# Order of products, refills, sums and decays in the first stage of a two-layer Mamba, FP4 and attention kernel

## The chip, the cores and the metric

The kernel runs on one core of one Trainium2 chip. The metric is the device time of one execution in microseconds; the time before is the median of three runs. One execution was taken by the hardware profiler, and all views of the profile come from it. A core has a matrix engine (PE, with its weight loads shown as PEld), a vector engine (DVE), an activation engine (ACT), a general engine (POOL) and a queue engine for transfers (SP). Each runs its own instructions in order and waits for the others by semaphores.

## The reference

The inputs are eight sequences of 512 tokens with 256 channels, all in fp32. Two layers follow each other; the change touches the first alone:

```
xn = layernorm(x)
x  = x + mamba(xn) + fp4_ffn(xn)          # first stage of the kernel
xn = layernorm(x)
x  = x + block_sparse_attention(xn) + local_transformer(xn)   # second stage
```

The Mamba block, for each sequence:

```
u, z  = split(xn @ W_in.T)                 # 512 channels each
u     = silu(causal_conv4(u) + conv_b)
dt, B, C = split(u @ W_xproj.T)            # 16 each
delta = softplus(dt @ W_dt.T + b_dt)
h[t]  = exp(delta[t] * A) * h[t-1] + delta[t] * u[t] * B[t]     # 16 states a channel
y[t]  = sum over states of h[t] * C[t]
out   = ((y + D * u) * silu(z)) @ W_out.T
```

The feed-forward block quantizes its input, its weights and its hidden layer to FP4 in blocks of 16 and returns to fp32: `down(fp4(silu(x @ Wg.T) * (x @ Wu.T)))` with 704 hidden channels.

## The kernel before

**Stages.** Two stages run one after the other, each with its own buffers. The first (lines 117 to 855) takes the eight sequences ("batches", b) through Mamba and feed-forward and writes x1 to memory; the second (from line 858) does the rest. In the first stage all engine instructions keep the order in which the program issues them (class `Ordered`, line 45).

**The scan loop.** The loop at line 826 counts steps g. A step handles two of the 16 states of one 128-channel chunk c, so a chunk takes 8 steps, a batch 32 (`STEPS`) and all batches 256. The work of one step:

- `fetch_c(g + 2)`: SP fetches two rows of C, spread over 128 partitions (three buffers, cb).
- `scan(g)`: DVE runs two scans of 512 tokens into hh (four buffers), from the decays da and the inputs bu.
- `decay(g + 2)`: ACT makes two decays da = exp(delta * A) (six buffers, three steps' worth).
- `inputs(g + 1)`, in odd steps alone: PE refills bu, by 16 small matrix products, for the next two steps. bu lies in PSUM and has one buffer, so the refill waits for the odd step's scans.
- `times_c(g)`: POOL multiplies hh by C.
- `sum_states(g)`: PE adds hh into y by 8 transposes with accumulation (PSUM, one buffer). Before, sums are issued in odd steps: that of g - 2 ahead of the strands and that of g - 1 behind them; the first one of a chunk comes later, in its even step.

**Strands.** All other work of the stage consists of generators that are advanced once per step by `step()` (line 800): `head` (layer norm, input projection, convolution, silu, x-projection, softplus; it makes the next batch ready), `ffn` (quantization and feed-forward), `z` and `finish` (the gate and the end of one chunk), `output`, and at the start the preparation of weights and tables. `begin` sorts them by rank: z and finish first, then output, the softplus chains and diagonals, head, ffn. `skewed` turns a list of stages into a pipeline over units: in one advance, each unit in flight does one stage. A stage is written as (function, tiles freed, tiles taken): products go to PSUM tiles of the pool pmm, of which there are three (`MM`), and a strand whose next advance would need more than three held tiles is passed over in that step.

**behind.** A function given to `behind` is kept in the list `late` and issued at the end of the same `step()`, when all strands have been advanced. The line-53 helper records every instruction, so the profile shows L53 for the first stage and the tiles tell the work apart: ps_in, cv (projection and convolution), ps_z, z (the gate), ps_dt, delta, du, e (softplus and delta * u), ps_gu, h (gate and up products of the feed-forward), ps_i, ht, ps_d (turning and the down product), q_ (quantization), ps_xp, xd (x-projection), ps_y, u (end of a chunk), ps_tr, xt, xqt (turned inputs).

**Readiness.** Before scan g the loop makes sure that the delta and du of step g + 2 are ready (`able`, line 815); as long as they are not, it advances the strands alone (line 831).

Of the kernel before, what the change touches and what calls it, by code (L numbers as in the profile page):

```python
# [9 lines left out]
FP = mybir.dt.float32  # L10
BF = mybir.dt.bfloat16
AF = mybir.ActivationFunctionType
# [5 lines left out]
P = 128  # L18
NB, L, D = 8, 512, 256
NT = L // P  # L20
KC = D // P
DI, NS, DR = 512, 16, 16
# [36 lines left out]
def tile_kernel(ctx: ExitStack, tc: tile.TileContext, a: dict, out: bass.AP):  # L59
# [57 lines left out]
    with ExitStack() as s0:  # L117
# [50 lines left out]
        def behind(f):  # L168


            late.append(f)
# [201 lines left out]
        def head(b):  # L373
# [41 lines left out]
            def project(c, _):  # L415
                ps = pmm.tile([P, L], FP, tag="mm", name="ps_in")
                for k in range(KC):
                    pe.matmul(
                        ps, w_in[:, k, c * P : (c + 1) * P], xt[:, k, :], start=(k == 0), stop=(k == KC - 1)
                    )  # L420
                cv = rot.tile([P, L], FP, tag="cv", bufs=2, name="cv")
                behind(lambda: act.activation(
                    cv, ps, AF.Identity, scale=conv_w[:, c, 3:4], bias=conv_b[:, c : c + 1]
                ))
                return ps, cv

            def tap(cv, ps, c, s):
                dve.scalar_tensor_tensor(
                    cv[:, s:], ps[:, : L - s], conv_w[:, c, 3 - s : 4 - s], cv[:, s:], ALU.mult, ALU.add
                )  # L430

            def taps(c, st):
                ps, cv = st
# [11 lines left out]

            while b - 3 in u_:
                yield 0, 0
            stages = [(project, 0, 1), (taps, 1, 0), tanh, silu]
            yield from skewed(range(NC - 2), stages, 2)
            while b - 2 in u_:  # L450
                yield 0, 0
# [46 lines left out]
            def rank(c):  # L498
                ps = pmm.tile([P, L], FP, tag="mm", name="ps_dt")
                pe.matmul(ps, w_dt[:, c * P : (c + 1) * P], xd, start=True, stop=True)  # L500
                behind(lambda: parts(c, ps))
                return ps

            def parts(c, ps):
                dt = delta[b, c] = w1.tile([P, L], FP, tag="delta", bufs=HELD, name="delta")
                w = du[b, c] = w1.tile([P, L], FP, tag="du", bufs=HELD, name="du")
                act.activation(dt, ps, AF.Relu, bias=b_dt[:, c : c + 1])
                act.activation(ps, ps, AF.Abs, bias=b_dt[:, c : c + 1])
                act.activation(ps, ps, AF.Exp, scale=-1.0)
                act.activation(w, ps, AF.Copy, bias=1.0)  # L510

            def rests(c, ps):
                e = rot.tile([P, L], FP, tag="e", bufs=3, name="e")
# [16 lines left out]
            def turned(c, _):  # L530
# [10 lines left out]
            by = pool if b else dve  # L541
            begin(diagonals(), 2)
            stages = [
                (lambda c, _: rank(c), 0, 1), (rests, 1, 0), logs, deltas, (turned, 0, 0, 1),
            ]
            for c in range(NC):
                k = b * NC + c - HELD
# [6 lines left out]
        def ffn(b):  # L554

            xn = made[b][0]

            def first(i, _):
                return xn[:, 2 * i : 2 * i + 2, :].rearrange("p t d -> p (t d)")

            scales, *stages = fp4_stages(P, 2 * D)
            yield from skewed(range(2), [lambda i, _: scales(i, first(i, _)), *stages], 3)
            yield 0, 0
            while b - 1 in busy:
                yield 0, 0
            busy.add(b)
            xqt = one.tile([P, KC, L], FP, tag="xqt", name="xqt")

            def turn_x(k, _):
                ps = pmm.tile([P, L], FP, tag="mm", name="ps_tr")  # L570
                for t in range(NT):
                    pe.transpose(ps[:, t * P : (t + 1) * P], xn[:, t, k * P : (k + 1) * P], ident)
                behind(lambda: act.copy(xqt[:, k, :], ps))

            yield from skewed(range(KC), [(turn_x, 0, 0, 1)], 1)
            quantized.add(b)
            n = FI // 2

            def product(t, w, cols):
                ps = pmm.tile([P, L], FP, tag="mm", name="ps_gu")  # L580
                for k in range(KC):
                    pe.matmul(
                        ps[:, :n], xqt[:, k, t * P : (t + 1) * P], w[:, k, cols],
                        start=(k == 0), stop=(k == KC - 1),
                    )
                return ps

            def gate_up(half):
                cols = slice(half * n, (half + 1) * n)

                def gate(t, h):
                    ps = product(t, w_g, cols)
                    behind(lambda: act.activation(h[:, cols], ps[:, :n], AF.Tanh))
                    return h, ps

                def up(t, st):
                    h, ps = st
                    dve.scalar_tensor_tensor(h[:, cols], h[:, cols], 1.0, ps[:, :n], ALU.add, ALU.mult)
                    if half and t == NT - 1:
                        busy.remove(b)  # L600
                    return h, product(t, w_u, cols)

                def both(t, st):
                    h, ps = st
                    dve.tensor_tensor(h[:, cols], h[:, cols], ps[:, :n], ALU.mult)
                    return h

                return gate, up, both

            def down(t, ht):  # L610
                ps = pmm.tile([P, L], FP, tag="mm", name="ps_d")
                for c in range(NI):
                    pe.matmul(ps[:, :D], ht[:, c, :], w_d[:, c, :], start=(c == 0), stop=(c == NI - 1))
                return ps

            def add(t, ps):
                x = xs[b]
                dve.tensor_tensor(x[:, t, :], x[:, t, :], ps[:, :D], ALU.add)

            def begin_(t, _):  # L620
                return gate0(t, q.tile([P, FI], FP, tag="q_src", bufs=4, name="h"))

            (gate0, up0, both0), (gate1, up1, both1) = gate_up(0), gate_up(1)
            stages = [
                (begin_, 0, 1), (up0, 1, 1), (lambda t, st: gate1(t, both0(t, st)), 1, 1), (up1, 1, 1), (both1, 1, 0),
                *fp4_stages(P, FI),
                *to_inner(lambda t: hts[t % 2]), (down, 0, 1), (add, 1, 0),
            ]
            for i, need in enumerate(skewed(range(NT), stages, 5)):
                if i == len(stages) - 6:  # L630
                    yield from own_x(b)
                yield need
            done(b)
# [106 lines left out]
        def z(b, c):  # L740
            yield 1, 1
            ps = pmm.tile([P, L], FP, tag="mm", name="ps_z")
            for k in range(KC):
                pe.matmul(
                    ps, w_in[:, k, DI + c * P : DI + (c + 1) * P], made[b][1][:, k, :],
                    start=(k == 0), stop=(k == KC - 1),
                )
            t = rot.tile([P, L], FP, tag="z", bufs=2, name="z")
            behind(lambda: act.activation(t, ps, AF.Tanh))
            yield 0, -1  # L750
            z_[b, c] = t
            dve.scalar_tensor_tensor(t, t, 1.0, ps, ALU.add, ALU.mult)
            through.add((b, c))
# [43 lines left out]

        ranks = {output: 1, head: 3, ffn: 4, fp4_weights: 5, rotary_tables: 5}

        def step():  # L800
            brief = 0
            for s, (peak, kept, *briefly) in list(active.items()):
                if held[0] + peak <= MM:
                    held[0] += kept
                    brief += sum(briefly)
                    active[s] = next(s, None)
                    if active[s] is None:
                        del active[s]
            for f in late:
                f()  # L810
            late.clear()
            held[0] -= brief
# [9 lines left out]
            fetch_c(k)  # L822
            decay(k)
        inputs(0)
        g = summed = 0
        while g < total or active or any(s >= g for s in starts):
            clock[0] = g
            for f, *args in starts.pop(g, []):
# [5 lines left out]
                fetch_c(g + 2)  # L834
            if now:
                scan(g)
            if g + 2 < total:
                decay(g + 2)
            if g % 2 and g + 1 < total:
                inputs(g + 1)  # L840
            while summed < min(g - 1, total):
                sum_states(summed)
                summed += 1
            if g % 2:
                gates = {g - (b * NC + c + 1) * (NS // 2) : (b, c) for b in range(NB) for c in range(NC)}
                for k, f in ((-3, z), (1, finish)):
                    if k in gates:
                        begin(f(*gates[k]), 0)
            step()
            if now:  # L850
                times_c(g)
            if g % 2 and 0 <= summed < min(g, total) and summed % (NS // 2):
                sum_states(summed)
                summed += 1
            g += 1


# [679 lines left out]
```

## Time and profile before

| what | value |
|---|---|
| device time, median of three runs | 3360.19 us (3358.26 to 3360.55) |
| device time of the profiled execution | 3363.26 us |
| its span, first to last instruction | 3361.3 us |
| mean granted TensorE clock | 0.948 |
| first scan starts, last scan ends | 49.7 and 1335.4 us |
| first load of x1 by the second stage | 1359.0 us |
| busy over the span: PE, DVE, ACT, POOL | 2984.9, 2263.7, 1562.5, 1545.1 us |

The costliest groups of the first stage, from the page (busy and mean per instruction; matrix products count two instructions in the trace for one in the program, except transposes):

| group | instructions | busy us | mean ns |
|---|---|---|---|
| POOL hh times C | 256 | 612.6 | 2401 |
| DVE scan hh | 512 | 592.3 | 1199 |
| ACT decay da | 512 | 338.4 | 715 |
| PE sums y | 2048 | 315.9 | 306 |
| PE refill bu | 4096 | 185.4 | 328 |

Busy times of PE overlap in the pipeline, so a group's mean is longer than its share of time: 16 instructions of a refill pass in 1.17 us at the quickest. A line of the view of waits gives the engine that waited and for what it would have gone on with, the releaser, the time in total, how often and the longest. A line of the timeline gives start, duration, engine, line, operation, result and inputs, shapes and number, and in brackets the idle time before it with its releaser.

### The profile page before, as it was taken

Reading aid. Unit: us, or ns where it says so; the run is one execution under the profiler, and the core shown is the slowest. Engines: PE = TensorE matmul, PEld = TensorE weight load, DVE = VectorE, ACT = ScalarE, POOL = GpSimd, SP = SyncE. Lnnn points to the kernel's source line nnn. Section 1 sums busy time; section 2 is a strip of 40 time slices with the busy share of each in tenths; the row PEclk is TensorE's granted clock in tenths of the full one; section 3 lists DMA queues with packets and bytes.
Section 4 is the critical chain, followed back from the end, with each engine's and each line's share of the span. In section 5 each row is a group of like instructions: output and inputs, shape, how many; then the busy total and the mean of one; then the engine's idle time right before and its main releaser. Section 6 shows DMA issues by size and latency. Waiting matters only on the chain.

```text
span 3361.3 us, 50387 instructions
## 1 busy us (share of the span) xinstructions
PE 2984.9 (89%) x19012; PEld 1836.9 (55%) x19012; DVE 2263.7 (67%) x4426; ACT 1562.5 (46%) x3399; POOL 1545.1 (46%) x1103
## 2 busy tenths in 40 slices
PE   5577798887888778899999999999999999999998
PEld 3455566665666566455555545545545545545545
DVE  6878787888888787556466566556557556556544
ACT  5464646474656553234244334334334434433533
POOL 2786777786868797223123123223213312312412
PEclk7778998998899998999999999999999999999999
DMA  3333333333333343210110111110110110110110
GB/s 111 111 104 108 117 104 124 119 117 117 114 120 109 118 138 118 85 50 35 46 49 35 46 54 37 48 50 32 65 34 32 65 34 32 65 33 32 59 34 7
DMA packets 93801, 244.42 MB, mean 73 GB/s; under 512 B 9848, under 2 KB 46712, under 8 KB 93560
## 3 DMA queue, kind: packets, MB, share of 16 engines
q1 hardware_dynamic: 92408, 237.01, 20.8%
q10 hardware_dynamic: 1152, 4.19, 0.3%
q8 instruction: 151, 2.47, 0.3%
q14 instruction: 90, 0.74, 0.1%
HBM read 231.48 MB, written 9.70 MB: 72 GB/s over the span
## 4 chain that ended last, share of the span: by engine, by line
PE 62%; DVE 17%; ACT 4%; issue 3%; POOL 2%; DMA 1%; DVEq 0%; POOLq 0%; ACTq 0%; SPq 0%
PE ps_qkv L1190 10%; DVE hh L53 6%; PE ps_g L1369 5%; PE ps_a L1369 4%; PE ps_wo L1333 3%; PE bu L53 3%; PE y L53 3%; PE lo L1303 3%; PE ps_y L1404 3%; PE ps_w L1387 3%; PE pt L1289 3%; PE ps_ls L1242 2%; PE ps_gu L53 2%; PE ps_st L1103 2%; DVE nm L1056 2%
## 5 line engine op out<-in xcount | busy, mean ns | idle before, releaser
L53 POOL TENSOR_TENSOR hh<-hh,cb 128x1024 f32<-128x1024 f32 x256 | 612.6, 2401 | 263.7 <-DVE hh L53 147.8
L53 DVE TENSOR_TENSOR_SCAN hh<-da,bu 128x512 f32<-128x512 f32 x512 | 592.3, 1199 | 65.3 <-PE bu L53 62.9
L53 PE MATMUL bu<-bd,du 32*128 32x128 f32 x4096 | 185.4, 328 | 253.7 <-DVE hh L53 240.5
L53 ACT ACTIVATE da<-delta,a_neg 128x512 f32<-128x512 f32 x512 | 338.4, 715 | 19.4 <-DVE hh L53 17.3
L53 PEld LDWEIGHTS bu<-bd,du 32*128 32x128 f32 x4096 | 158.3, 226 | 310.4 <-issue 207.5
L53 PE MATMUL y<-ident,hh 128*128 128x128 f32 x2048 | 315.9, 306 | 7.0 <-ACT delta L53 6.4
L1280 POOL TENSOR_TENSOR pr<-pr,lrs 128x512 f32<-128x512 f32 (+1 forms) x256 | 234.9, 934 | 177.4 <-DVE lrs L1278 137.6
L53 PEld LDWEIGHTS y<-ident,hh 128*128 128x128 f32 x2048 | 266.5, 158 | 55.7 <-issue 27.3
L1209 POOL TENSOR_TENSOR r<-r,r 128x512 f32<-128x512 f32 x128 | 163.0, 1273 | 285.4 <-DVE r L1207 242.9
L1261 ACT ACTIVATE pr<-ps_ls,nm 128x256 f32<-128x256 f32 (+1 forms) x512 | 222.0, 449 | 122.9 <-DVE nm L1255 116.7
L1205 DVE TENSOR_TENSOR r<-ps_qkv,tab 128x512 f32<-128x512 f32 x128 | 88.2, 689 | 200.1 <-ACT sq L1204 198.1
L1107 ACT ACTIVATE pt_e<-ps_st 128x512 f32<-128x512 f32 x320 | 166.8, 597 | 107.4 <-PE ps_st L1101 101.2
L945 POOL MEMSET sa<- 128x1 f32 x16 | 1.6, 99 | 449.9 <-DVE sf L1391 356.9
L1375 ACT ACTIVATE gl<-ps_g,b 128x512 f32<-128x512 f32 x96 | 65.9, 687 | 305.8 <-PE ps_g L1369 305.8
L1150 POOL TENSOR_TENSOR x1s<-x1s,bsum 128x256 f32<-128x256 f32 x32 | 23.2, 725 | 371.8 <-DVE x1s L1149 371.8
L1255 DVE CUSTOM_DVE_ANT_0 ps_ls<-ps_ls,mask 128x256 f32<-128x256 f32 (+1 forms) x512 | 184.1, 421 | 6.7 <-PE ps_ls L1242 5.8
L1369 PE MATMUL ps_g<-hn,wf 128*128 128x512 f32 x384 | 184.7, 604 | 4.0 <-DVE hn L1358 2.6
L1190 PE MATMUL ps_qkv<-wqkv,sf 128*128 128x512 f32 x384 | 182.4, 608 | 0.0
L1190 PE MATMUL ps_qkv<-wqkv,s 128*128 128x512 f32 x384 | 180.7, 606 | 0.0
L1376 DVE SCALAR_TENSOR_TENSOR ht<-ps_a,b,gl 128x512 f32<-128x512 f32 x80 | 60.0, 750 | 157.5 <-PE ps_a L1369 157.5
L1289 PE MATMUL pt<-ident,pr 128*128 128x128 f32 x896 | 131.3, 282 | 32.8 <-POOL pr L1280 28.1
L1369 PE MATMUL ps_a<-hn,wf 128*128 128x512 f32 x320 | 150.4, 592 | 0.0
(225 smaller groups left out, 6324.6 us busy)
## 6 DMA issues: line engine op xcount, KB each, us to landing
cb<-c_d SPq DMA_DIRECT2D x256, 512.0 KB, 3.7
wqkv<-in_wqkv SPq DMA_DIRECT2D x16, 1536.0 KB, 7.3
wf<-in_wf SPq DMA_DIRECT2D x16, 1408.0 KB, 6.3
wf<-in_wf SPq DMA_DIRECT2D x16, 768.0 KB, 4.7
tab<-tab SPq DMA_DIRECT2D x16, 512.0 KB, 3.5
wo<-in_wo SPq DMA_DIRECT2D x16, 512.0 KB, 3.7
xl<-in_x SPq DMA_DIRECT2D x8, 512.0 KB, 4.7
x<-in_x SPq DMA_DIRECT2D x8, 512.0 KB, 4.4
```

Source lines behind the costliest of these rows:

```text
L53: return self.tc.keep_in_program_order(getattr(self.engine, name)(*args, **kwargs))
L1107: act.activation(pt, banks[g], AF.Exp)
L1190: pe.matmul(ps, shifted(s, k, t * P, P), wqkv[:, k, i * IN : (i + 1) * IN], start=(k == 0), stop=(k == KC - 1),)
L1209: pool.tensor_tensor(r1[:, i], r1[:, i], r2, ALU.add)
L1255: last = dve.tensor_tensor_reduce(at, at, msk[:, 2 * P - nk :], -1.0, 3e38, ALU.add, ALU.min, nm[:, i : i + 1])
L1261: act.activation(pr[:, at], banks[r][:, at], AF.Exp, bias=nm[:, i : i + 1], scale=-1.0, accum_out=rs[:, i : i + 1],)
L1280: pool.tensor_tensor(ph, ph, rs.unsqueeze(2).to_broadcast([P, 2, nk]), ALU.mult)
L1289: pe.transpose(pt[:, j * P : (j + 1) * P], pr[:, j * P : (j + 1) * P], ident)
L1303: pe.matmul(o[r * LD : (r + 1) * LD, i * P : (i + 1) * P], lv[:, keys[j], h * LD : (h + 1) * LD], prts[r][:, (i * nkt + j) * P : (i * nkt ...
L1333: pe.matmul(ps, wo[:, c, m * P : (m + 1) * P], ot[:, c, :], start=(c == 0), stop=(c == IN // P - 1),)
L1369: pe.matmul(dst, wf1[:, k, off : off + P], hn[:, k, :], start=(k == 0), stop=(k == KC - 1))
L1387: pe.matmul(ps, wf2[:n, c, m * P : (m + 1) * P], ht[c][:n], start=(c == 0), stop=(c == NHC - 1),)
```

## The change

Five things change, all in the first stage.

1. Five activations that were issued `behind` their products, in the same step, become stages of their own: the first tap of the convolution (`tap0`), the softplus's four activations (`parts`), the tanh of both gate halves (`tanh0`, `tanh1`) and the tanh of z. They are issued one step after the product, and the DVE operation that frees the PSUM tile one step later than before.
2. In a step of the scan loop the strands are advanced directly after `scan(g)`, ahead of the refill `inputs(g + 1)` and of the sums.
3. The decays of step g + 2 are issued after the strands' own instructions and ahead of the functions in `late` (through the new argument `between`).
4. Every step g issues the sum of step g - 2, at its end, behind `times_c(g)`.
5. `finish` begins at k = 2, one step later; both z and finish are looked for in every step.

```diff
                     pe.matmul(
                         ps, w_in[:, k, c * P : (c + 1) * P], xt[:, k, :], start=(k == 0), stop=(k == KC - 1)
                     )
-                cv = rot.tile([P, L], FP, tag="cv", bufs=2, name="cv")
-                behind(lambda: act.activation(
-                    cv, ps, AF.Identity, scale=conv_w[:, c, 3:4], bias=conv_b[:, c : c + 1]
-                ))
-                return ps, cv
+                return ps
...
+            def tap0(c, ps):
+                cv = rot.tile([P, L], FP, tag="cv", bufs=2, name="cv")
+                act.activation(
+                    cv, ps, AF.Identity, scale=conv_w[:, c, 3:4], bias=conv_b[:, c : c + 1]
+                )
+                return ps, cv
...
-            stages = [(project, 0, 1), (taps, 1, 0), tanh, silu]
+            stages = [(project, 0, 1), tap0, (taps, 1, 0), tanh, silu]
...
             def rank(c):
                 ps = pmm.tile([P, L], FP, tag="mm", name="ps_dt")
                 pe.matmul(ps, w_dt[:, c * P : (c + 1) * P], xd, start=True, stop=True)
-                behind(lambda: parts(c, ps))
                 return ps
...
-                (lambda c, _: rank(c), 0, 1), (rests, 1, 0), logs, deltas, (turned, 0, 0, 1),
+                (lambda c, _: rank(c), 0, 1), parts, (rests, 1, 0), logs, deltas, (turned, 0, 0, 1),
...
                 def gate(t, h):
-                    ps = product(t, w_g, cols)
-                    behind(lambda: act.activation(h[:, cols], ps[:, :n], AF.Tanh))
-                    return h, ps
+                    return h, product(t, w_g, cols)
+
+                def tanh(t, st):
+                    h, ps = st
+                    act.activation(h[:, cols], ps[:, :n], AF.Tanh)
+                    return st
...
-                (begin_, 0, 1), (up0, 1, 1), (lambda t, st: gate1(t, both0(t, st)), 1, 1), (up1, 1, 1), (both1, 1, 0),
+                (begin_, 0, 1), tanh0, (up0, 1, 1), (lambda t, st: gate1(t, both0(t, st)), 1, 1), tanh1, (up1, 1, 1), (both1, 1, 0),
...
+            yield 0, 0
             t = rot.tile([P, L], FP, tag="z", bufs=2, name="z")
-            behind(lambda: act.activation(t, ps, AF.Tanh))
+            act.activation(t, ps, AF.Tanh)
             yield 0, -1
...
-        def step():
+        def step(between=lambda: None):
...
                     if active[s] is None:
                         del active[s]
+            between()
             for f in late:
                 f()
...
             if now:
                 scan(g)
-            if g + 2 < total:
-                decay(g + 2)
+            gates = {g - (b * NC + c + 1) * (NS // 2) : (b, c) for b in range(NB) for c in range(NC)}
+            for k, f in ((-3, z), (2, finish)):
+                if k in gates:
+                    begin(f(*gates[k]), 0)
+            step(lambda: g + 2 < total and decay(g + 2))
             if g % 2 and g + 1 < total:
                 inputs(g + 1)
-            while summed < min(g - 1, total):
-                sum_states(summed)
-                summed += 1
-            if g % 2:
-                gates = {g - (b * NC + c + 1) * (NS // 2) : (b, c) for b in range(NB) for c in range(NC)}
-                for k, f in ((-3, z), (1, finish)):
-                    if k in gates:
-                        begin(f(*gates[k]), 0)
-            step()
             if now:
                 times_c(g)
-            if g % 2 and 0 <= summed < min(g, total) and summed % (NS // 2):
-                sum_states(summed)
-                summed += 1
+            if 0 <= g - 2 < total:
+                sum_states(g - 2)
             g += 1
```

More of the change, by code (lines that the diff above doesn't have):

```diff
@@ L510, in parts @@
                 act.activation(w, ps, AF.Copy, bias=1.0)
+                return ps
             def rests(c, ps):
@@ L606, in both @@
                     return h
-                return gate, up, both
+                return gate, tanh, up, both
             def down(t, ht):
@@ L621, in begin_ @@
                 return gate0(t, q.tile([P, FI], FP, tag="q_src", bufs=4, name="h"))
-            (gate0, up0, both0), (gate1, up1, both1) = gate_up(0), gate_up(1)
+            (gate0, tanh0, up0, both0), (gate1, tanh1, up1, both1) = gate_up(0), gate_up(1)
             stages = [
-                (begin_, 0, 1), (up0, 1, 1), (lambda t, st: gate1(t, both0(t, st)), 1, 1), (up1, 1, 1), (both1, 1, 0),
+                (begin_, 0, 1), tanh0, (up0, 1, 1), (lambda t, st: gate1(t, both0(t, st)), 1, 1), tanh1, (up1, 1, 1), (both1, 1, 0),
                 *fp4_stages(P, FI),
@@ L824, in tile_kernel @@
         inputs(0)
-        g = summed = 0
+        g = 0
         while g < total or active or any(s >= g for s in starts):
```

## The prediction

> **What bounds the kernel now.** I read first the slices of the page, to find the stage that the change touches.
>
> ```profile
> PE   5577798887888778899999999999999999999998
> DVE  6878787888888787556466566556557556556544
> ACT  5464646474656553234244334334334434433533
> POOL 2786777786868797223123123223213312312412
> PEclk7778998998899998999999999999999999999999
> ```
>
> A slice is 84 us. The change lies in the first 16, where no engine is full: DVE stands highest, PE and POOL beside it, and the granted TensorE clock is below full. From slice 17 on PE is at 9 and the clock is full; nothing of the change reaches there. Next, the busy time of the stretch that holds the scans and of its tail (columns: stretch, length, busy PE, PEld, DVE, ACT, POOL, clock, DMA, GB/s).
>
> ```profile
> 47.40:1338.00 1290.60, 1008.17 (x8214) 771.94 (x8215) 1067.69 (x1272) 726.98 (x1189) 982.98 (x564) 0.89 0.34 115
> 1338.00:1361.00 23.00, 19.29 (x104) 15.71 (x102) 9.72 (x17) 4.91 (x10) 11.60 (x13) 1.00 0.09 21
> ```
>
> DVE works 1067.7 of 1290.6 us, so 222.9 us are idle, and DVE issues in program order: the stage lasts as long as DVE's work plus DVE's waits. The third view says what these waits are (us in total, times, longest), for DVE in that stretch, and for PE over the run:
>
> ```profile
> DVE hh L53 <- PE bu L53: 62.9, 59, 2.4
> DVE h L53 <- ACT h L53: 47.5, 23, 3.7
> DVE e L53 <- ACT du L53: 32.7, 21, 3.3
> DVE cv L53 <- ACT cv L53: 25.4, 15, 3.2
> DVE x L53 <- PE ps_d L53: 15.7, 14, 1.9
> DVE z L53 <- ACT z L53: 10.2, 11, 3.2
> DVE h L53 <- PE ps_gu L53: 4.0, 7, 2.1
> DVE bd L53 <- PE ps_bt L53: 2.7, 3, 1.3
> ...
> PE bu L53 <- DVE hh L53: 240.5, 90, 12.0
> ```
>
> The rows h, e, cv and z are the pattern "product, activation behind it in the same step, DVE in the next": 47.5 + 32.7 + 25.4 + 10.2 = 115.8 us. The first row is the refill of bu, which an odd step issues for the next two scans; today DVE waits little for it, because PE stands ready at it (last row: PE is the one that waits). The timeline shows one such place.
>
> ```profile
> 664.93 0.49 DVE L53 TENSOR_TENSOR h<-h,ps_gu 128x352 f32<-128x352 f32 x1
> 665.16 1.17 PE L53 MATMUL bu<-bd,du 32*128 32x128 f32 x32 [1.38 <-DVE hh L53]
> ...
> 666.49 2.33 DVE L53 TENSOR_TENSOR_SCAN hh<-da,bu 128x512 f32<-128x512 f32 x2 [1.06 <-PE bu L53]
> ...
> 690.50 2.09 PE L53 MATMUL bu<-bd,du 32*128 32x128 f32 x32 [2.36 <-DVE hh L53]
> ```
>
> The bu tile has one buffer: a refill starts at the odd scans' end, takes 1.17 us (2.09 where the clock is low), and the next scan follows at once if DVE has too little of its own to do meanwhile.
>
> **The change, part by part.** All instructions stay; their order and their step change. The counts below are from the order in which the two built programs issue their instructions, with what each waits for. Durations are rows of the trace.
>
> *(a) Activations a step behind their products.* DVE's operation now comes two steps after the product, its activation one. The 115.8 us go. I take -100, because ACT still ends each step on copies of products of that step (du, ht, xt) and may hand some of it on. Ends: -116 and -50.
>
> *(b) Products ahead of the refill.* PE issues in order. In an odd step it now runs all strands' products before the refill; the sums and the next step's products queue behind. A product that waits for a DVE operation of its own step (it takes the PSUM tile that this operation frees) holds the refill. In the changed order 50 of 124 odd steps have such a product ahead of the refill. Step 161 shows it: after the scans DVE has one operation (e, 0.68 us); ps_d's six matmuls wait for it (2.59 us in the before's rows), then comes the refill (1.17): it ends 4.44 us after the scans, DVE is done after 0.68, and waits 3.76. In the old order the refill is first and ends at 1.17. I did this sum for every odd step (mean DVE durations; products 0.68 us for a ps_gu instruction, 0.43 for ps_d, 0.47 for ps_o, 0.94 for ps_in and ps_z, 1.02 for ps_dt, 0.60 for four transposes; only the products from the first blocked one on count): DVE's waits come to 21.7 us in the old order, where the trace has 62.9, and to 125.5 us in the new one, in 89 steps, with a mean end of 2.34 us. The sum is low because the mean refill is 185.4 / 128 = 1.45 us, not 1.17, 24% more. 24% of 2.34 is 0.56, times 89 is 50: 125.5 + 50 = 175, less the 62.9 of today, +113. Ends: +63 (the bare sum) and +213 (the steady odd steps 131 to 163 sum to 27.1, 1.6 each; 2.16 with the 0.56, times 128 is 276, less 62.9).
>
> The low clock is seen in the two refills above, 1.17 and 2.09 us. The Trainium skill, page "TensorE: Matmul & The Clock Gate", part 1, says that the array runs at half clock after an idle window of about 3.4 us and at full clock after a busy one; by that rule shorter idle gaps of PE would speak for the change, and with all refills at 1.17 the +113 would be +63.
>
> *(c) PSUM tiles held longer.* project, rank, z and both gates now keep their tile for two steps instead of one; the stage has three tiles, and a strand whose turn finds none skips a step. The built order shows the result: the x-projection of later batches comes 3 to 9 steps later (step 120 instead of 111 for batch 4, 212 instead of 207 for batch 7), and at steps 30, 94 and 126 the next batch's du is not ready, so 3, 1 and 4 steps of the strands alone are issued with no scan in them. I walked the four at step 126: from the end of scan 125 the softplus chain (two rounds of four activations of 0.6, Ln between two table loads of 1.28, three POOL operations of 1.28, transposes, copy) lasts about 14.5 us, in which DVE has 9.5 us of work: 5 idle. The three at 30 alike, 2 for the one: +12. Ends: +5, and +32 (eight times 4 us, nothing covered).
>
> "Perfetto Trace Analysis" of the skill, section "Optimization Strategy", says that a bubble that repeats can mean too little PSUM for the next tile; it speaks against holding tiles longer, and has no price.
>
> *(d) The tail.* The same lag makes the loop end at step 275 instead of 265: ten more steps of the feed-forward strand after the last scan. The ten of today last 23 us with 9.7 us of DVE work: 2.3 a step, 1.3 idle. Ten more: +14 (their DVE work is taken out of the loop). Ends +5 and +26.
>
> *(e)* Start before the first scan, pipeline one stage deeper in two places: +2 (0 to +5).
>
> *(f) Other waits of DVE for products of the step before* (ps_d, ps_gu, ps_bt and smaller, 25 us with those not shown): products start earlier, but queue behind others: -5 (-25 to +15).
>
> *(g) At nothing.* The decays go behind the strands' activations: a scan needs them two steps on, and ACT is busy 56%; were that cover gone, each late pair costs up to its 1.33 us. Three more table loads (80 for 77) lie there too, 3.8 us if bare. The copy of y and the finish move a step back: the first sum of the next channel waits for that copy in its own (even) step, where no refill is due; bare, some 1 us at 32 places. sums at g - 2 instead of pairs: the h tile has four buffers, so a scan needs the sum issued two steps before. SP's fetches of C keep their place; the store of x on ACT's queue and the x load on SP's move with the lag and are waited for by the sum of x alone.
>
> Sum: -100 + 113 + 12 + 14 + 2 - 5 = +36 us on the span of 3361.3: 3397; the median of the runs, 3360.2, lies 1.1 lower: **3396 us**.
>
> **Rivals.** *The refill fits (faster).* PE idles 240 us at the refill today and would use it for the products, so the refill is late only by the bare sum: -116 + 63 + 5 + 5 - 25 = -68, 3292, at best; -100 + 63 + 12 + 14 + 2 - 5 = -14, 3346, with the middle values of the rest; 3320 between them. For it: PE's idle time and the low clock. Against: the 50 blocked steps, where PE can't run ahead. It decides where DVE's waits for bu stay below 62.9 + 77 = 140 us, since all other terms make -77.
>
> *The refill becomes the chain (much slower).* PE, late from the even step's blocked products, is late at every odd one: (b) at +213, +136 in all, 3496. For it: the steady batches, where 15 of 17 odd steps are late by the sum; PE busy 78% of the stretch already. Against: early batches show less.
>
> *A wash.* (a) and (b) cancel and (c) and (d) are covered: within 0.2%, 3353 to 3367, about what a measurement of this kernel can tell from no change.
>
> **How the numbers follow.** Forecast, 3367 to 3440: 0.50. Much slower: 0.20. Refill fits: 0.25. Wash: 0.05. Faster 0.25, same 0.05, slower 0.70. The range leaves out the lower half of the faster case and the upper half of the much slower one: 3320 to 3490. The likeliest case's own range is 3367 to 3440.
>
> **What would show it.** DVE's waits for ACT's h, du, cv and z under 20 us in all (a); its wait for PE's bu between 140 and 220 us (b), with PE waiting less at bu and more at products for DVE; du late at the batch changes of the first batches only (c); some 23 us more between the last scan and the second stage's first load (d). Wrong I am if bu stays below 140 us, or if waits for ACT stay.

## The result and the profile after

The changed kernel takes 3476.23 us (median of four runs, 3474.44 to 3477.64), the one before 3360.37 beside it: ratio 1.0345 (1.0327 to 1.0363). The forecast was slower, 3396 us with a range of 3320 to 3490: the sign was right and the time lies in the range, but the loss is +116 us where +36 was forecast. The profiled execution has a span of 3473.8 us, 112.5 more than before.

| stretch of the span, us | before | after | change |
|---|---|---|---|
| first scan to last scan's end | 1285.7 | 1369.7 | +84.0 |
| from there to the second stage's first load of x1 | 23.6 | 51.1 | +27.5 |
| second stage | 2002.3 | 2003.3 | +1.0 |

The slices of the page after (86.8 us each):

```profile
PE   5567777787777788799999999999999999999998
DVE  6978776777677778565655655565466556556544
PEclk7788998998899899989999999999999999999999
```

The first stage now fills nearly all of slice 17, where it ended a sixth into it before, and DVE shows mostly sevens where it had sevens and eights. The busy time of the two first-stage stretches of the table, after (columns as in the prediction):

```profile
47.40:1419.40 1372.00, 1035.65 (x8152) 744.32 (x8152) 1059.55 (x1252) 728.74 (x1181) 970.65 (x557) 0.89 0.33 108
1419.40:1470.50 51.10, 38.77 (x165) 29.62 (x164) 20.22 (x34) 8.10 (x20) 20.78 (x19) 0.90 0.08 23
```

DVE is busy 1059.6 us in the loop (1066.8 before, in the same stretch up to its last scan) and idle 312.4 (221.2 before). So the loop's +84 is +91 of waits, less 7 of work that moved into the tail. The granted clock of the loop is 0.89 as before: PE doesn't run slower. DVE's waits in the loop, after:

```profile
DVE hh L53 <- PE bu L53: 227.9, 91, 6.1
DVE x L53 <- PE ps_d L53: 15.5, 6, 6.0
DVE hh L53 <- ACT da L53: 13.7, 5, 6.2
DVE e L53 <- ACT du L53: 10.4, 5, 4.9
DVE z L53 <- ACT z L53: 9.5, 2, 6.0
...
DVE h L53 <- ACT h L53: 1.6, 2, 0.9
```

The four rows of ACT that the shift was to remove fell from 115.8 to 21.5 us (cv is gone). The wait for the refill rose from 62.9 to 227.9, and further scans (the row hh <- ACT da and smaller ones) wait 35.0 us where they waited 2.2; what these rows are is taken up under (g). PE's waits over the run show the other side:

```profile
PE bu L53 <- DVE hh L53: 70.5, 30, 9.3
PE ps_gu L53 <- DVE h L53: 30.5, 18, 3.8
...
PE ps_in L53 <- DVE cv L53: 25.2, 8, 4.0
PE ps_gu L53 <- DVE x L53: 13.4, 9, 5.4
...
PE ps_d L53 <- DVE z L53: 12.9, 5, 5.0
```

PE waited 240.5 us at the refill before, 70.5 now. In exchange the stage's products wait, for DVE, ACT and POOL: between 47 and 1440 us, all such rows of PE, without those of the sums, come to 260 us, and to 24 before. 214 of the 260 are waits for DVE. The releasers (h, cv, x, z) are mostly not inputs of the product that waits: they are the DVE operations that read the PSUM tile that it takes over. One such place, from the timeline after:

```profile
1011.85 1.95 PE L53 MATMUL ps_in<-xt,w_in 128*128 128x512 f32 x4 [2.26 <-DVE u L53]
...
1012.65 2.32 DVE L53 TENSOR_TENSOR_SCAN hh<-da,bu 128x512 f32<-128x512 f32 x2
...
1013.86 1.35 PE L53 MATMUL ps_gu<-w_g,xqt 128*128 128x352 f32 x4
...
1015.04 1.04 PE L53 MATMUL y<-ident,hh 128*128 128x128 f32 x8
...
1015.92 2.76 PE L53 MATMUL ps_d<-w_d,ht 128*128 128x256 f32 x12
...
1018.60 1.17 PE L53 MATMUL bu<-bd,du 32*128 32x128 f32 x32
...
1019.94 2.33 DVE L53 TENSOR_TENSOR_SCAN hh<-da,bu 128x512 f32<-128x512 f32 x2 [4.97 <-PE bu L53]
```

In the even step ps_in waits 2.26 us for DVE. That makes ps_i (in a line left out), ps_gu and the sum late, so that PE only comes to the even step's sum (y) as the odd step's scans end, at 1014.97 (1012.65 + 2.32). Then follow the odd step's six products ps_d, which wait for nothing, then the refill, 3.6 us after the scans. DVE waits 4.97 us. In the old order the refill stands ahead of these sums and of ps_d.

### The profile page after: what moved, and what is told of

Its sections match the earlier page's. It is cut to its first block, busy times and chain, and to the rows that moved or that the text cites. A ratio compares the mean times of both kernels' runs of the same rounds, so it can differ in the third digit from the quotient of the medians.

```text
span 3473.8 us, 50299 instructions
## 1 busy us (share of the span) xinstructions
PE 3033.5 (87%) x19012; PEld 1823.8 (53%) x19012; DVE 2267.7 (65%) x4426; ACT 1567.8 (45%) x3402; POOL 1543.3 (44%) x1103
## 4 chain that ended last, share of the span: by engine, by line
PE 58%; DVE 14%; ACT 3%; issue 2%; POOL 1%; DMA 0%; DVEq 0%; ACTq 0%; POOLq 0%
PE ps_qkv L1191 10%; PE ps_g L1370 5%; DVE hh L53 5%; PE ps_a L1370 4%; PE ps_wo L1334 3%; PE lo L1304 3%; PE ps_y L1405 3%; PE ps_w L1388 3%; PE pt L1290 2%; PE ps_gu L53 2%; PE bu L53 2%; PE ps_ls L1243 2%; PE y L53 2%; DVE nm L1057 2%; PE pt_qk L1182 1%
## 5 line engine op out<-in xcount | busy, mean ns | idle before, releaser
L53 DVE TENSOR_TENSOR_SCAN hh<-da,bu 128x512 f32<-128x512 f32 x512 | 592.5, 1201 | 263.2 <-PE bu L53 227.9
L53 PE MATMUL y<-ident,hh 128*128 128x128 f32 x2048 | 300.6, 295 | 8.8 <-ACT delta L53 8.7
L53 PEld LDWEIGHTS y<-ident,hh 128*128 128x128 f32 x2048 | 254.5, 153 | 57.9 <-issue 31.4
L53 PE MATMUL bu<-bd,du 32*128 32x128 f32 x4096 | 171.1, 310 | 71.3 <-DVE hh L53 70.5
L53 PEld LDWEIGHTS bu<-bd,du 32*128 32x128 f32 x4096 | 145.1, 211 | 128.6 <-issue 92.6
```

The lines of the kernel that those rows point to most:

```text
L53: return self.tc.keep_in_program_order(getattr(self.engine, name)(*args, **kwargs))
```

## The experiments

Ratios are to the kernel before, run beside each on the same chip, with 95% intervals.

**The order and the shift, separately.** Four kernels fill a table of two questions: do the five activations come a step behind, and where does the refill stand?

*The change with the refill first again:*

```diff
             if now:
                 scan(g)
+            if g % 2 and g + 1 < total:
+                inputs(g + 1)
...
             step(lambda: g + 2 < total and decay(g + 2))
-            if g % 2 and g + 1 < total:
-                inputs(g + 1)
```

> The changed kernel with one move undone: the refill of bu is issued ahead of the strands again; activations a step behind, decays and sums stay as changed. Theory A (the products ahead of the refill are the cost: DVE waited 227.9 us for bu in the changed kernel, 62.9 before): DVE's wait for bu falls to 60 to 110 us, and the time by 110 to 160 us, to 3315 to 3365 us. Theory B (the longer hold of PSUM tiles is the cost: 8 steps without scans, 10 more tail steps, later batches): all of that is still there, the time stays above 3440 us. Theory C (the late sums and decays are the cost): they are still there too, the time stays above 3440 us, and waits move from bu to da and hh.

*The change with the five activations behind their products again* (order alone):

```diff
-                return ps
+                cv = rot.tile([P, L], FP, tag="cv", bufs=2, name="cv")
+                behind(lambda: act.activation(
+                    cv, ps, AF.Identity, scale=conv_w[:, c, 3:4], bias=conv_b[:, c : c + 1]
+                ))
+                return ps, cv
...
-            stages = [(project, 0, 1), tap0, (taps, 1, 0), tanh, silu]
+            stages = [(project, 0, 1), (taps, 1, 0), tanh, silu]
```

and in the same way for `parts`, `tanh0`, `tanh1` and z.

> The changed kernel with the five activations put back behind their products; products ahead of the refill, decays behind, one sum a step, finish at k = 2 stay. The built order has no step without scans and ends at step 266. Theory A: DVE's wait for bu is 140 to 220 us and its waits for ACT's h, du, cv and z are back at some 115 us, so the time is 3440 to 3500 us. Theory B: near the kernel before, 3350 to 3380 us.

*The kernel before with the five activations a step behind* (shift alone): the change's edits to the stage lists and to z, with the old `step()` and the old loop.

> The kernel before with the five activations a step behind their products and nothing else; refill, sums and decays in the old order. The built order has 3 steps without scans at each of steps 30, 126, 158, 190 and 222, and ends at step 276. Theory A: waits for ACT's h, du, cv and z fall from 115 to under 30 us, bu stays under 110 us, some 28 us more tail and 20 us for the steps without scans: 3310 to 3370 us. Theory B: 3430 us or more.

*Both edits undone at once:* refill first, activations behind. What stays of the change is the place of sums and decays and the later finish.

> The changed kernel with both undone: activations behind their products again and the refill first; what is left of the change is one sum a step behind the strands, the decays behind the strands, finish at k = 2. Theories A and B: within 15 us of the kernel before, 3345 to 3375 us. Theory C: 3400 us or more.

| order of the step | activations behind | a step later | price of the shift |
|---|---|---|---|
| as before | 3361.94 (before) | 3328.60, 0.9903 (0.9888 to 0.9917) | -33 |
| change, refill first | 3343.89, 0.9948 (0.9932 to 0.9965) | 3361.25, 0.9993 (0.9981 to 1.0005) | +17 |
| change, products first | 3404.34, 1.0129 (1.0114 to 1.0144) | 3476.23, 1.0345 (1.0327 to 1.0363) | +72 |

DVE's wait for bu is 91.3 and 100.3 us in the second row, 175.9 and 227.9 in the third, 55.4 for the shift alone. So putting the products ahead of the refill costs 60 us without the shift and 115 with it: that is the loss, and the two other theories, which expected over 3440 for the refill put first, fell. The shift lengthens the tail, from the last scan to the second stage's first load, by 24 to 27 us in every row. The loop, from the first scan to the last, becomes 68 us shorter by it in the old order and 10 shorter in the second row, but 42 longer in the third, where the refill stands behind products. Three expectations missed. The order alone was to bring the 115 us of waits for ACT back and to take 3440 us or more; the waits were about 19 (e 9.8, z 5.2, the others 2 each), so the shift isn't needed to lose them in that order. The shift alone was to bring them under 30 us; 52 were left. And the kernel with both undone came in just below its range; there these waits are 56 us, 37.4 of them those of e.

**What of the order holds the refill: the length of PE's queue, or the products' waits?** If the number of instructions ahead of the refill counted, taking half of the sums away would help. The changed kernel and, as a control, the kernel before, each with half the sums:

```diff
-            for i in range(2):
+            for i in range(1):
...
-                        start=(n + i + t == 0), stop=(n + i == NS - 1 and t == NT - 1),
+                        start=(n + i + t == 0), stop=(n + i == NS - 2 and t == NT - 1),
```

> The changed kernel with half of the sums left out: only the first of a step's two states is added into y (four transposes a step instead of eight, some 0.5 us of TensorE a step), so the output lacks every second state. Nothing else moves. Theory Q (the refill is late because TensorE has too much queued ahead of it when the odd scans end): in front of each refill lie the sums of the two steps before it, so the refill comes up to 1 us earlier; DVE's wait for bu falls from 227.9 us to 110 to 160 us and the time by 60 to 120 us, to 3355 to 3415 us. Theory P (the refill is late because products ahead of it wait in place for a DVE operation of their own step): DVE's operations come when they came, the wait for bu stays above 200 us and the time above 3450 us.

> The control: the kernel before with the same half of the sums left out. There TensorE stands waiting at the refill, so both theories expect little: 3330 to 3360 us.

The changed kernel stayed at 3476.54, 1.0333 (1.0311 to 1.0355); the kernel before gained, 3334.65, 0.9911 (0.9891 to 0.9931). The wait of the changed kernel with half the sums:

```profile
DVE hh L53 <- PE bu L53: 237.3, 92, 7.5
```

It didn't fall, although PE had 122 us less of sums to do (y: 300.6 busy us, now 178.7). PE's waits for products rose from 260 to 322 us. The test is weaker than it was meant to be: the granted clock of the loop fell too (last section), and PE's busy time in the same stretch went down by 69 us, not 122. That speaks against the queue's length as the cause, and the next experiment, which leaves the queue as it is, decides.

**More tiles.** The direct test gives the pool pmm more PSUM tiles with the order unchanged, so that a product needn't wait for DVE's operation of its own step. To make room for them, the refill was cut to two row strips (half of the inputs are left out, and both steps of a pair scan the same two states), in a control with three tiles, in one with five, and in the kernel before with five. The rule `MM = 3`, which decides what a step issues, stays.

```diff
-        pmm = s0.enter_context(tc.tile_pool(name="pmm0", bufs=MM, space=PSUM))
+        pmm = s0.enter_context(tc.tile_pool(name="pmm0", bufs=5, space=PSUM))
...
-            bu = spreads[g] = spreads[g + 1] = pbu.tile([P, 4, NT, P], FP, tag="bu", name="bu")
+            bu = spreads[g] = spreads[g + 1] = pbu.tile([P, 2, NT, P], FP, tag="bu", name="bu")
             for t in range(NT):
-                for r in range(4):
+                for r in range(2):
...
-                    hs[g][:, i, :], decays[g][i], bu[:, 2 * (g % 2) + i :: 4], 0.0, ALU.mult, ALU.add
+                    hs[g][:, i, :], decays[g][i], bu[:, i::2], 0.0, ALU.mult, ALU.add
```

> A control for the next run: the changed kernel with a refill of two of the four row strips, so that bu takes two PSUM banks instead of four (8 small products instead of 16, on two strips side by side, so the refill should last as long as it did); both steps of a pair scan the same two states, and half of the inputs are left out. The strands still have three PSUM tiles, and the order of all else is the changed kernel's. Both theories: 3450 to 3490 us, wait for bu 200 to 240 us.

> The same with the two freed banks given to the strands: five PSUM tiles, while the rule that holds a strand back still counts three, so that the order of instructions stays the changed kernel's. In the built order 7 odd and 9 even steps have a product that waits for a DVE operation of its own step, 56 and 69 in the control. Theory P (products that wait in place for DVE, in odd and in even steps, hold the refill): TensorE's waits for products (256 us in the changed kernel) fall under 100 us, DVE's wait for bu under 130 us, and the time by 70 to 130 us against the control. Theory Q (the queue of products and sums is too long in itself): bu stays above 180 us and the time within 30 us of the control.

> The kernel before with the same small refill and five tiles. Its products stand behind the refill, where little waits for them: within 30 us of the kernel before, 3330 to 3375 us.

The control takes 3488.52 us, 1.0373 (1.0352 to 1.0394); with five tiles it is 3359.69, 0.9995 (0.9986 to 1.0005), 129 us less from this one edit. The kernel before with five tiles is 3374.34, 1.0036 (1.0023 to 1.0049): no gain against the kernel before with the full refill and three tiles. What the small refill alone does in the old order wasn't run; the changed kernel was 12 us slower with it. PE's waits in the control:

```profile
PE bu L53 <- DVE hh L53: 60.4, 31, 6.7
PE ps_gu L53 <- DVE h L53: 30.6, 16, 3.9
PE ps_in L53 <- DVE cv L53: 25.2, 8, 4.1
```

and with five tiles, where ps_du for POOL, an input of its own, is the first product in the list:

```profile
PE bu L53 <- DVE hh L53: 169.0, 71, 9.6
PE ps_du L53 <- POOL du L53: 23.8, 12, 3.9
```

DVE's wait for bu with five tiles:

```profile
DVE hh L53 <- PE bu L53: 107.7, 67, 4.7
```

It was 210.3 in the control. The waits for DVE to free a tile are gone from the top of PE's list, its waits for products fall from 252 to 70 us in all, PE waits at bu again, and DVE's wait halves. In the built order the steps with a product that waits for a DVE operation of its own step fall from 125 (56 odd, 69 even) to 16. With the small refill and five tiles in both, the change is 15 us faster than the old order (3359.7 against 3374.3).

**The gates' two stages.** The shift gives the feed-forward strand two stages more for each token tile. The changed kernel without these, and the old order with the other three shifts only:

```diff
                 def gate(t, h):
-                    return h, product(t, w_g, cols)
+                    ps = product(t, w_g, cols)
+                    behind(lambda: act.activation(h[:, cols], ps[:, :n], AF.Tanh))
+                    return h, ps
...
-                (begin_, 0, 1), tanh0, (up0, 1, 1), (lambda t, st: gate1(t, both0(t, st)), 1, 1), tanh1, (up1, 1, 1), (both1, 1, 0),
+                (begin_, 0, 1), (up0, 1, 1), (lambda t, st: gate1(t, both0(t, st)), 1, 1), (up1, 1, 1), (both1, 1, 0),
```

> The changed kernel with the two gate tanh put back behind their products; first tap, softplus and the tanh of z stay a step behind. The built order ends at step 266 instead of 275 and has 3 steps without scans instead of 8. If the tail and the lag come from the feed-forward's two added stages, the stretch from the last scan to the second stage's first load falls from 51 to some 26 us; the refill still stands behind the products (the sum over odd steps gives 117 us instead of 125), so the wait for bu stays at 190 to 230 us: 3425 to 3455 us. If the lag also makes the wait for bu: 3410 us or less, as with no shift at all (3404).

> The kernel before (old order) with first tap, softplus and the tanh of z a step behind their products, the gates' tanh as before. The shift alone gave 3329 us with a tail of 50 us. If that tail is the gates' alone, it is 24 to 26 us here, the waits of h for ACT come back in part: 3310 to 3335 us. If the shift's gain is the gates' (h has the largest wait, 47.5 us): 3345 us or more.

The first takes 3425.87 us, 1.0181 (1.0164 to 1.0198): 50 less than the changed kernel, of which the tail gives 25 (25.8 us, from 51.1); bu waits 186 us, just under what was expected. The second takes 3314.20, 0.9852 (0.9837 to 0.9867), with a tail of 23.7 us and 54.7 us of waits for bu in the loop.

**A faster version.** The second of these with the decays after the strands, the change's third edit:

```diff
-            if g + 2 < total:
-                decay(g + 2)
...
-            step()
+            step(lambda: g + 2 < total and decay(g + 2))
```

> The fastest so far (old order, first tap, softplus and the tanh of z a step behind, gates as before; 3314 us) with the decays behind the strands' activations as in the changed kernel. If the late decays are what removes h's wait for ACT in the changed kernel, the 48 us that are left of these waits fall under 25: 3285 to 3310 us. If that was the sums' place, nothing moves: 3305 to 3325 us.

3294.63 us, 0.9799 (0.9782 to 0.9815): the fastest of all, some 18 to 20 us below the same kernel with the decays ahead and 67 below the one before. The waits for ACT's h, e, cv and z fell from 47.7 to about 39 us, less than the "under 25" that was hoped for; h's own, which the expectation was about, didn't fall (23.0, now 25.7), e's did. So these waits are only part of the gain, and where the rest of it lies isn't shown. The wait for bu kept its size:

```profile
DVE hh L53 <- PE bu L53: 51.0, 53, 2.4
```

## Why the prediction was half right

| term of the sum, us | predicted | measured in the span |
|---|---|---|
| (a) waits for ACT's h, e, cv, z | -100 | -94 |
| (b) wait for the refill | +113 | +198 (+165 in the row bu, +33 in other rows, see (g)) |
| (c) steps without scans | +12 | 14, inside the other rows |
| (d) tail | +14 | +27.5, less 7 of DVE's work out of the loop: +20 |
| (e) start | +2 | 0 |
| (f) waits for other products | -5 | -8 |
| (g) decays and the rest | 0 | 0 |
| second stage, other rows | 0 | -4 |
| sum | +36 | +112 |

**(a) was right in size, and its reason only in part.** The 94 us went, but the order alone removes about as much (19 us left of 115.8, against 52 for the shift alone). The working gave them all to the shift. With both undone, where neither the shift nor the products' place is changed, 56 are left: the place of sums and decays takes some 60 by itself, and the products ahead of the refill some 37 more. Why they do isn't shown.

**(b) is the step that failed: its mechanism was right, its size was not.** It was put at +113 and measures +198; these 85 us make the miss of 76, less the 12 of (c), which lie inside other rows, and some small differences. "Products ahead of the refill", held by PSUM tiles that DVE frees in the same step, is what costs: the refill put first and the five tiles show it. But the working counted "only the products from the first blocked one on", in odd steps, as if PE stood free when the odd scans end. By the profile after, 269 us lie between the odd scans' end and the refill, in 127 pairs of steps (60 before): 63 until PE is through with the even step's sum, 206 for the odd step's own products and their waits; in only 50 of the 269 is PE idle. The rest is products that run, with the refill and the scan behind them. The place shown first is of this kind: nothing waits in the odd step, but the even step's product did, and every later product is late with it.

The built order had said so: 64 even steps have a product that waits for a DVE operation of their own step, and 55 odd ones (all such products counted; the working had 50). Of 260 us that scans after a refill wait, 157 follow the blocked odd steps; 67 follow the 41 odd steps that have no such product but come after a blocked even step, and 36 the other 32. The working's sum came to 125 for all of them.

The sum had also shown that it lacked something: for the old order it gave 21.7 us where the trace has 62.9. The working put this down to slow refills and added 24%. But 59 refills that are 0.28 us slower make 17 of the 41 us, and the mean refill then got shorter, 171.1 / 128 = 1.34 us, from 1.45. The lower end, +63, set the new order's sum against the old order's trace; sum against sum it is +104.

The rival "the refill becomes the chain" named the right reason ("late from the even step's blocked products") and priced (b) at +213, near the +198. Its time, 3496 us, is 20 from the measured one, which lies above the likeliest case's own range of 3367 to 3440; it lies in the full range because that takes in half of this rival.

**(c)** In the three places with strands alone, steps 30, 94 and 126, DVE idles 7.8, 2.9 and 8.6 us ahead of the scan, 19.3 in all and 4.9 before: 14 more, 12 forecast.

**(d)** The tail is longer by the two stages that the shift gives the gates: without them it is 25.8 us. Its idle time grew by 16 us (14.8 to 30.9), about the 14 forecast, but its DVE work by 11.5, of which only 7 are missed in the loop. Waits of DVE in the tail, after:

```profile
DVE x L53 <- PE ps_d L53: 12.4, 3, 5.5
DVE h L53 <- PE ps_gu L53: 5.6, 2, 3.6
```

With no scans left to fill it, the feed-forward strand's chain is bare there.

**(g) was rightly put at nothing, though the view of waits says otherwise.** By the releasers that it names, scans waited 2.2 us for things other than bu before and 35.0 after, in 17 places, 13.7 us of it for "ACT da". But 15 of the 17 scans, with 34.1 us, start 0.14 to 0.17 us after the end of a refill, as those of the row bu do (0.165 in the median), and their own decays had been done for 3 us or more. The longest of them, from the timeline after:

```profile
1249.45 1.34 ACT L53 ACTIVATE da<-delta,a_neg 128x512 f32<-128x512 f32 x2
...
1254.84 1.26 DVE L53 TENSOR_TENSOR bd<-four,ps_bt 128x512 f32<-128x512 f32 x2
...
1256.15 4.92 PE L53 MATMUL ps_d<-w_d,ht 128*128 128x256 f32 x12 [0.89 <-DVE bd L53]
...
1259.80 2.55 ACT L53 ACTIVATE da<-delta,a_neg 128x512 f32<-128x512 f32 x4
...
1261.00 1.17 PE L53 MATMUL bu<-bd,du 32*128 32x128 f32 x32
...
1262.34 2.33 DVE L53 TENSOR_TENSOR_SCAN hh<-da,bu 128x512 f32<-128x512 f32 x2 [6.25 <-ACT da L53]
```

The scans at 1262.34 are those of step 220. Their decays are the two at 1249.45, done more than 11 us before; the four at 1259.80 are for the next two steps. The refill ends at 1262.17 (1261.00 + 1.17), 0.17 us ahead of the scans. It stands behind ps_d, which waits 0.89 us for DVE (bd) and then takes 4.92 us at a granted clock of 0.56, where the same six products took 2.76 us at a clock of 1.00 in the place shown first. So these 34.1 us are part of (b), as are 1.1 of the 2.2 before, and about 1 us is left of (g) in both kernels. Counted by the refill's end, DVE's waits for it are 64 us before and 262 after; 58 in the shift alone, 94 with both undone, 114 with the refill first and 200 in the order alone; 257 in the control with the small refill and 137 with five tiles. The order of the kernels, and so the reading of the experiments, stays the same.

**PSUM and the clock.** Two tiles are worth 129 us in the changed order; in the old one, where PE's products wait only 24 us, no gain was seen. The Trainium skill's page "Perfetto Trace Analysis", section "Optimization Strategy", reads a repeating bubble as a possible sign of too little PSUM; the runs agree. The clock, to which the prediction gave 50 us of its range, doesn't make the difference: the granted clock of the loop is 0.89 in both kernels.

**What stays open.** How the blocked time divides among the kinds of tiles, and how much of the lost ACT waits the sums' place brings and how much the decays', wasn't tried: only the decays' place was changed by itself, in the old order. Five tiles with the full refill, and the small refill in the old order with three tiles, weren't run.

## What to carry to other kernels

A product that takes over a buffer freed in the same step must not stand, on an engine that issues in order, ahead of what the freeing engine will need next: give it a buffer more, or let the needed one go first. When such holds are priced, carry an engine's lateness from one step into the next; a sum step by step that starts each with a free engine came to 125 us here where the profile has 262. Where a view names a releaser that the waiting operation doesn't read, look at what ended just before it started. Putting an operation a step later is not free either: it holds its buffer for a step more and makes the last pass through the pipeline longer, here by 25 us for two stages.

## What was not expected of the hardware

With half the sums taken away, the changed kernel's PE did less and ran at a lower granted clock: the same stretch as above, with half the sums:

```profile
47.40:1419.40 1372.00, 966.59 (x7090) 649.90 (x7091) 1053.95 (x1243) 726.23 (x1176) 963.43 (x554) 0.85 0.32 107
```

0.85 where the whole kernel had 0.89: 13% fewer instructions (7090 for 8152) brought only 6.7% less busy time (966.6 for 1035.7 us). The Trainium skill's rule quoted in the prediction ("TensorE: Matmul & The Clock Gate", part 1: the array runs slower after idle windows) agrees in direction: PE's idle time in this stretch rose from 336 to 405 us. In the kernel before, half the sums lowered the clock of the loop less, from 0.89 to 0.87. And a refill cut from four row strips to two kept its time: at the quickest 1.16 us for 16 instructions, 1.17 for 32, and in all 174.2 busy us for 2048 with five tiles, 171.1 for 4096 in the changed kernel. So the strips' products run side by side.
